# Four cross-attention layers under a planned order: rank tables of their own for the first and last batch, and two weight slabs transferred earlier

## The chip, the cores and the metric

The kernel runs on one core of a Trainium2 chip. The metric is the device time of one execution in microseconds (us). The engines are TensorE (PE, with its weight loads listed apart as PEld), VectorE (DVE), ScalarE (ACT), GpSimd (POOL) and SyncE (SP, whose queue issues the transfers).

## The reference

Four cross-attention layers in a row are applied to `x` (16 batches of 100 rows, 256 wide), each with the same context `ctx_1024` (16 batches of 361 rows, 256 wide) and 16 heads. All numbers are float32. Cut to what matters:

```python
# L0: heads of 16, layer norm on both sides, then a feed-forward
qn, kn = layer_norm(x, ln1), layer_norm(ctx, ln1)
x = x + softmax((qn @ wq + bq) (kn @ wk + bk)^T / 4) (kn @ wv + bv) @ wo + bo
x = x + gelu(layer_norm(x, ln2) @ w1 + b1) @ w2 + b2
# L1: heads of 64, rms norm on the query alone, no scale, raw context
x = x + softmax((rms(x) @ wq) (ctx @ wk)^T) (ctx @ wv) @ wo
# L2: heads of 64, rotary embedding of q and k, a mask on the keys, layer norm after the sum
x = layer_norm(x + softmax(mask(rope(x @ Wq) rope(ctx @ Wk)^T / 8)) (ctx @ Wv) @ Wo)
# L3: heads of 16, layer norm on both sides
x = x + softmax((ln(x) @ Wq + bq) (ln(ctx) @ Wk + bk)^T / 4) (ln(ctx) @ Wv + bv) @ Wo + bo
```

## The kernel before

The kernel is a list of works that is ordered on the host and then written out. For each of the 16 batches the function `batch(b)` adds some 561 works to a `Plan`: the context transposed (`keys_T`: `cT` raw, `zT` normalised), layer L0 (`small_heads_layer`), `feed_forward`, L1 and L2 (`large_heads_layer`), L3 (`small_heads_layer` again), and the store. Each work is one or several instructions of one engine, or of either ACT or DVE where an estimate may choose (`copied`). An attention layer goes in four units of four heads: `scores` on PE (L839), the row maximum on DVE (L894, or L888 and L891 with a mask), the exponential on ACT (L900), the reciprocal on DVE (L864), the division on POOL (L871), the transposes of the probabilities on PE (L935), their copy from PSUM on ACT or DVE (L614, L616), and the weighted sum on PE (L733).

PE works have a tile shape, called mode in the code: `col32` (four strips of 32 columns abreast: nearly all products, L733), `row64` (transposes by halves of 64 rows, and the scores of L1 and L2), `row32` (the scores of L0 and L3), and None (whole array: the folding of norm weights into projection weights at the start, L519 and L568, and one transpose at L487).

`Plan.order` walks through time by its own estimates. Of all works whose inputs are ready it picks the one that starts earliest; equal starts go by rank. A PE work of another mode than PE's present one counts `keep[mode]` ns later while the present run of that mode is shorter than `run[mode]` ns, and earlier by `pull` times the PE work at hand in its mode:

```python
w.rank = w.batch * ORDER["lag"] - w.tail
if w.batch >= 0:
    w.rank = w.rank + ORDER["batch"][w.batch] + ORDER["place"][w.place]
...
if engine == "PE" and start < free_at["PE"] + ORDER["window"]:
    m = mode if set_now else w.modes[0]
    at_hand[m] = at_hand.get(m, 0.0) + busy
```

Here `start` is never before `free_at["PE"]`, `place` is the number of the work within its batch, and `tail` the longest chain of estimates behind it. What comes out is a fixed order of instructions for each engine, buffers and PSUM banks included. Each engine then runs its own list strictly in that order and waits wherever an input is late.

The transfers at the start are a chain (`load`, `load_const`, `load_slab`, `load_inputs`): SP issues them in the order in which they are written. The weights come as 12 slabs of 1 MB: 0 is L0's four projections, 1 and 2 are `w1` and `w2`, 3 to 6 are L1's wq, wk, wv and wo, 7 to 10 L2's, 11 L3's four. `rows` are five bias and norm rows, `cst` the rotary tables, `crow` the column vectors. Each slab is issued at L426; the context at L398 and L402, into one buffer `ctxr` that all batches share; `x` at L403; the mask at L416. Two works wait for `rows` early: the addition at L574 on DVE, and through it the first residual row of L0 on POOL (L1000).

Of the kernel before, what the change touches and what calls it, by code (L numbers as in the profile page):

```python
# [18 lines left out]
B, S, E = 16, 100, 256  # L19
# [12 lines left out]
for _name, _w in (  # L32
# [11 lines left out]
SLABS = (  # L44
    ("L0_xattn_wk", "L0_xattn_wv", "L0_xattn_wq", "L0_xattn_wo"),
    ("L0_xattn_w1",), ("L0_xattn_w2",),
    ("L1_xattn_wq",), ("L1_xattn_wk",), ("L1_xattn_wv",), ("L1_xattn_wo",),
    ("L2_xattn_Wq",), ("L2_xattn_Wk",), ("L2_xattn_Wv",), ("L2_xattn_Wo",),
    ("L3_xattn_Wq", "L3_xattn_Wk", "L3_xattn_Wv", "L3_xattn_Wo"),
)  # L50

ORDER = {
    "lag": 329100, "pull": 7.0, "window": 0,
    "keep": {None: 5720, "row64": 350, "row32": 60, "col64": 4920, "col32": 4770},
    "run": {None: 0, "row64": 22810, "row32": 33110, "col64": 63830, "col32": 0},
    "batch": (-388000, 3000, 0, 0, 0, 0, 0, 0, 0, 0, 0, 0, 0, 0, 75500, -1018000),
    "place": [  # L60
        100 * k for k in (
        1788, 2147, 158, -655, -3660, -3678, -2864, -2202, 107, -3757, -3737, -2474, -6828,
        -7159, -6429, -769, -7090, -5897, -2734, -7751, -4511, -3850, -6654, -4642, -4482,
        -5346, -1898, 2595, -228, -444, -1077, -3621, -2420, -4476, -6306, -9158, -8069, -6006,
        -6446, -5152, -5925, -9187, -6281, -10716, -8043, -8908, -6734, -8414, -9577, -12471,
        -5956, -6155, -10918, -12687, -6524, -7417, -6968, -2206, -1022, -442, -455, -1136,
        -2296, -853, -1376, -601, -1207, -1840, 1341, -965, -1984, -3436, -983, -70, -1962,
        -308, -474, -1148, -2199, -415, 539, -44, -2289, -1348, -2217, -2483, 1649, -1589, -48,
        696, 1885, -105, 1108, -3136, 2296, 2261, -5257, -5446, -5535, -7310, -2216, -2756,
        -1279, -3966, 91, 72, -2289, -1637, -3654, -1230, -2781, -1130, 3999, 260, -460, -3123,  # L70
        -3075, -3185, 46, 1463, -4241, -4207, -2879, 377, -1894, -1072, -1487, -4901, -3613,
        -5484, -4750, -2583, -4378, -3249, -684, 1881, -2295, 6, -4275, -2714, -1398, -1067,
        104, 878, -633, -877, -70, 4307, -129, -1409, -7268, -876, -534, 37, 274, 2712, 2005,
        667, -383, 2192, 1954, -1158, -2545, -4879, -1718, 1071, 6135, 6999, 3972, 2354, 3233,
        1740, 23, 3538, 2458, 5060, -3364, -1285, -1996, -3442, -1454, -1733, 3264, -2782,
        -8386, 850, -638, -3875, -3486, -3922, -4750, -4633, -2049, -6108, -1229, -2781, -3686,
        -1451, -1172, -737, 2568, 1316, 5887, 2353, 432, 1063, 3355, 1611, 6911, 3359, -1272,
        471, 758, -3387, -4259, -244, -1565, -733, -1162, -665, 1469, -5644, -2369, -2467,
        -1133, -3934, -4444, -2937, -6670, -5590, -8380, -10655, -6731, -4637, -5076, -4059,
        -3451, -4805, -5454, -3113, -4724, 2806, -3339, 2422, 3428, 807, 2546, -23, -641, 1012,  # L80
        1005, 534, 5580, 2620, 1990, 1001, -1243, 1291, 4604, 5568, 3408, 842, -954, -3671,
        -2620, 85, -856, -4166, -9442, -5661, -1103, -588, -3921, -3608, -3730, 492, 1219, -144,
        392, 2013, 4590, 7120, 8002, 4805, 4640, -42, 3885, 3005, 5141, 3205, 3474, 4285, 5881,
        6503, 4010, 5003, 4359, 6006, 5431, 5577, 3067, 4246, 8605, 3685, 7642, 6505, 1444,
        2688, 1704, 373, 3065, -2188, 66, -2348, -3742, -576, 1795, -1133, -123, 353, 1264,
        -186, -3119, -6662, 3188, -2888, -2292, 639, -2200, -544, 3192, -2158, 268, 3976, 6005,
        2305, 2809, 1883, -2100, 3932, 3267, 4051, 4427, 5327, 5654, 6007, 7398, 1836, 4762,
        1273, 3327, 1747, 1882, 5151, 1055, 1284, -952, -703, -2974, -2900, 925, -4076, -1021,
        3029, -3569, 89, -700, -1127, 2089, -1480, 2484, 2990, 2248, -1452, 494, 2456, 841,
        -1167, -472, -998, -1941, -4850, -2206, -2817, -3790, -5666, -3510, -1965, -2311, -5292,  # L90
        -5354, -4528, -6920, -7546, -6247, -4195, -347, -1590, -2503, -5174, -5611, -2342, -254,
        -6432, -5406, -3715, -714, -1257, 679, 1808, 3757, -507, 2782, 93, 1915, 1124, -2501,
        -1632, 2528, -5366, -1885, -3098, -7585, -9522, -10769, -8421, -11233, -6607, -8773,
        -9422, -2724, -3769, -4192, -4443, -4468, -5791, -4103, -3810, -781, -5155, -2771, 414,
        -1459, -2334, -1027, -2813, -5985, -3939, -7212, -3270, -4409, -2012, -4946, -5630, 827,
        -6312, -1161, -2028, -1786, 1600, -917, -2390, 1068, 1539, 3314, -634, 3761, 2764, 6969,
        3668, -5275, -1551, -1593, -5718, -3450, 3167, 4367, 4831, 5443, 6356, 3460, 376, -1230,
        -2843, -2595, -4621, -6268, -4694, -2912, -1704, -2369, -634, -4432, -993, -2880, -899,
        -428, -4599, -6793, -2902, -6740, -6610, -2330, -263, 2256, 1828, 1882, 1805, 1066,
        4514, 1473, 739, -2476, -1257, -3998, 2747, 713, 4018, 3384, 4954, 2476, 1679, -3033,  # L100
        -682, -1921, -1131, 4768, 1129, 1216, -1441, 3923, 4051, 1136, 3547, 1612, 1261, -4001,
        -3191, -1679, 691, -338, 6706, 4913, 3905, 4065, -504, 145, -2018, -654, -6952, -1397,
        -1334, -2478, -1894, -1645, -2680, 241, 934, 1107, 1565, -3853,
        )
    ],
}


# [43 lines left out]
class Plan:  # L152
# [62 lines left out]
    def order(self):  # L215
# [6 lines left out]
        for w in self.work:  # L222
            w.rank = w.batch * ORDER["lag"] - w.tail
            if w.batch >= 0:
                w.rank = w.rank + ORDER["batch"][w.batch] + ORDER["place"][w.place]
        free_at = {e: 0.0 for e in ("PE", "ACT", "DVE", "POOL", "SP")}
        mode, run, table = None, 0.0, None
        ready = sorted((w.rank, w.index) for w in self.work if not w.n_after)
# [4 lines left out]
        while len(done) < len(self.work):  # L233
            held, able, at_hand = set(), [], {}
            for _, i in ready:
                w = self.work[i]
# [22 lines left out]
                for e, occ, lat in w.engines:  # L259
# [5 lines left out]
                    if cost is None or s + lat < cost - 1:  # L265
                        engine, cost, start, busy = e, s + lat, s, occ
                if engine == "PE" and start < free_at["PE"] + ORDER["window"]:
                    m = mode if set_now else w.modes[0]
# [12 lines left out]
            _, start, end, w, e, occ, set_now = best  # L281
            if e == "PE":
                run = run + occ if set_now else occ
# [34 lines left out]
def tile_xattn_layers(  # L318
# [65 lines left out]
    plan = Plan(slots)  # L384
# [27 lines left out]
    def load_mask(b):  # L412
        mu = plan.buf("mask", f"mask_{b}")

        def issue(_):
            nc.sync.dma_start(out=mu.ap, in_=mask[b : b + 1, :].to_broadcast([P, SK]))  # L416

        if b < 1:
            load([("SP", 200.0, 4000.0)], issue, [mu])
        else:  # L420
            plan.add([("SP", 100.0, 4000.0)], issue, writes=[mu])
        return mu

    def load_const(dst, src, us, name):
        b = plan.buf(None, name)
        load([("SP", us * 1e3, us * 1e3 + 3000.0)], lambda _: nc.sync.dma_start(out=dst, in_=src), [b])  # L426
        return b

    w, slab_of = {}, {}

    def load_slab(i, pieces=1):
        t = const.tile([P, 2048], F32, name=f"slab{i}")
        names = SLABS[i]
        n, wide = len(names), 2048 // pieces
        for k in range(pieces):
            cols = slice(k * wide, (k + 1) * wide)
            part = load_const(t[:, cols], slabs[i, :, cols], 2.5 / pieces, f"slab{i}_{k}")
            for name in names[k * n // pieces : (k + 1) * n // pieces]:
                slab_of[name] = part
        for k, name in enumerate(names):  # L440
            part = t[:, k * (2048 // n) : (k + 1) * (2048 // n)]
            kc = 8 if n == 1 and name[-2:].lower() in ("wo", "w2") else 2
            w[name] = part.rearrange("p (c n) -> p c n", c=kc)
# [5 lines left out]
    loads, masks = {}, {}  # L449
# [4 lines left out]
    crow_b = load_const(crow, colvecs, 0.1, "crow")  # L454
    load_slab(0, 2)
    cst_b = load_const(cst, consts, 1.0, "cst")
    rows_b = load_const(rows, rowvecs.partition_broadcast(P), 1.7, "rows")
    plan.batch = 0
    masks[0] = load_mask(0)
    plan.batch = -1  # L460
    load_slab(1)
    plan.batch = 1
    loads[1] = load_inputs(1, 1000.0, 5000.0)
    plan.batch = -1
    for i in range(2, len(SLABS)):
        load_slab(i)
    row = {name: rows[:, i, :] for i, name in enumerate(ROWS)}
    parity = cst[:, 0:2]
# [932 lines left out]
```

## Time and profile before

| what | value |
|---|---|
| median of 3 runs | 1950.47 us (1947.33 to 1952.12) |
| the profiled execution | 1949.26 us, span 1947.5 us |
| instructions | 99714 |
| PE busy | 1920.4 us (99%) in 43881 matmuls |
| DVE, ACT, POOL busy | 1294.9, 1179.8, 1048.2 us |
| mean granted clock of PE | 0.994 |
| read from memory | 21.92 MB |

The span is the time from the first to the last instruction; some 1.8 us lie around it. "Idle before" is the time in which an engine stood still before an instruction, with what ended it. The granted clock is PE's share of its full clock in a stretch. A busy PE in this page is one with a matmul anywhere in flight, so a change of tile shape, in which the array empties, counts as busy.

### The profile page before, as it was taken

What the parts mean: (1) busy time and instruction counts of PE and PEld (TensorE: products, weight loads), DVE (VectorE), ACT (ScalarE), POOL (GpSimd) and SP (SyncE); (2) the same over time, 40 slices, a digit from 0 to 9 for tenths busy, and PEclk for the clock granted to TensorE, in tenths of its full rate; (3) what the DMA queues carried; (4) which work ended last, traced back from release to release, by engine and by line L of the source; (5) the groups of instructions that cost most, each with busy time, mean ns of one, the idle gap of its engine ahead of it and who ended that gap; (6) DMA issues with size and microseconds to landing.
All of it is one profiled execution on the core that took longest, in us unless ns stands there. A gap on an engine that the chain in (4) does not pass through costs nothing.

```text
span 1947.5 us, 99714 instructions
## 1 busy us (share of the span) xinstructions
PE 1920.4 (99%) x43881; PEld 1272.2 (65%) x43881; DVE 1294.9 (66%) x4497; ACT 1179.8 (61%) x3425; POOL 1048.2 (54%) x1680
## 2 busy tenths in 40 slices
PE   8999999999999999999999999999999999999997
PEld 4666666575766757667575675767667576675756
DVE  5556666666676666667666676666676666775766
ACT  4646656675665756656566566655666466565636
POOL 5354455555556555455645555455555555555564
PEclk9999999999999999999999999999999999999997
DMA  7000000000000000000000000000000000000000
GB/s 303 3 3 14 5 12 8 3 14 5 12 8 3 14 5 14 5 3 15 5 14 5 12 8 3 15 5 12 8 3 15 5 12 7 3 15 4 4 3 7
DMA packets 14730, 29.94 MB, mean 15 GB/s; under 512 B 3362, under 2 KB 12376, under 8 KB 12888
## 3 DMA queue, kind: packets, MB, share of 16 engines
q1 hardware_dynamic: 14296, 23.56, 3.7%
q8 instruction: 344, 5.64, 1.2%
q14 instruction: 90, 0.74, 0.1%
HBM read 21.92 MB, written 1.64 MB: 12 GB/s over the span
## 4 chain that ended last, share of the span: by engine, by line
PE 94%; DVE 3%; POOL 2%; DMA 1%; issue 0%; ACT 0%; SPq 0%; POOLq 0%; DVEq 0%; ACTq 0%
PE ps L733 68%; PE ps L839 13%; PE ps L935 10%; DVE prob L894 2%; POOL prob L871 1%; PE ps L674 1%; PE ps L761 1%; DMA slab<-slabs_dram 1%; DMA mask<-mask_dram 0%; ACT prob L900 0%; PE ps L716 0%; SPq L426 0%; DVE prob L888 0%; DVE pT L616 0%; DVE two L891 0%
## 5 line engine op out<-in xcount | busy, mean ns | idle before, releaser
L871 POOL TENSOR_SCALAR prob<-prob,two 100x361 f32<-100x361 f32 x1024 | 568.6, 573 | 607.9 <-DVE two L864 384.8
L900 ACT ACTIVATE prob<-prob,two 100x361 f32<-100x361 f32 x1024 | 603.0, 593 | 124.3 <-DVE prob L894 73.8
L894 DVE TENSOR_SCALAR_CACHE_REDUCE prob<-ps 100x361 f32<-100x361 f32 x768 | 374.7, 531 | 171.9 <-PE ps L839 112.5
L733 PE MATMUL ps<-slab,cT 128*32 128x512 f32 (+1 forms) x3072 | 366.6, 595 | 0.0
L733 PE MATMUL ps<-cT,slab 128*32 128x361 f32 x4096 | 344.6, 468 | 0.7 <-DMA slab<-slabs_dram 0.7
L839 PE MATMUL ps<-kT,qT 32*100 32x181 f32 (+3 forms) x4096 | 303.7, 329 | 1.4 <-ACT pT L614 0.9
L935 PEld LDWEIGHTS ps<-ident,prob 36*128 36x128 f32 (+1 forms) x6144 | 216.0, 139 | 95.7 <-POOL prob L871 43.5
L614 ACT COPY pT<-ps 128x384 f32<-128x384 f32 (+1 forms) x508 | 223.6, 493 | 88.5 <-PE ps L935 69.5
L839 PEld LDWEIGHTS ps<-kT,qT 32*100 32x100 f32 (+1 forms) x4096 | 228.7, 164 | 72.6 <-issue 42.1
L935 PE MATMUL ps<-ident,prob 36*128 36x36 f32 (+1 forms) x6144 | 243.0, 227 | 7.7 <-POOL prob L871 7.2
L614 ACT COPY v<-ps 128x512 f32<-128x512 f32 (+1 forms) x131 | 76.6, 585 | 268.1 <-PE ps L733 163.5
L616 DVE COPY pT<-ps 128x384 f32<-128x384 f32 (+1 forms) x260 | 146.4, 575 | 134.3 <-PE ps L935 131.2
L733 PEld LDWEIGHTS ps<-cT,slab 128*32 128x32 f32 x4096 | 122.9, 109 | 148.5 <-issue 132.9
L900 ACT ACTIVATION_READ_ACCUMULATOR prob<-prob,two 100x1 f32 x1024 | 194.6, 190 | 0.0
L733 PEld LDWEIGHTS ps<-slab,cT 128*32 128x32 f32 (+1 forms) x3072 | 86.0, 107 | 140.0 <-issue 127.9
L888 DVE TENSOR_TENSOR prob<-ps,cap 100x361 f32<-100x361 f32 x256 | 125.7, 527 | 65.2 <-PE ps L839 41.0
L792 POOL TENSOR_TENSOR sw<-sw,rot 128x361 f32<-128x361 f32 x128 | 105.5, 825 | 105.3 <-DVE sw L788 102.3
L733 PE MATMUL ps<-pT,v 128*32 128x100 f32 (+1 forms) x6144 | 155.5, 250 | 2.7 <-DVE pT L616 2.3
L733 PEld LDWEIGHTS ps<-pT,v 128*32 128x32 f32 (+1 forms) x6144 | 136.3, 110 | 25.1 <-issue 12.3
L800 POOL TENSOR_TENSOR kT<-kT,sw 128x361 f32<-128x361 f32 x128 | 122.9, 961 | 6.0
L733 PE MATMUL ps<-xT,slab 128*32 128x100 f32 x5120 | 124.4, 250 | 1.5 <-DVE xT L696 1.0
L891 DVE TENSOR_REDUCE two<-prob 100x1 f32<-100x361 f32 x256 | 124.7, 518 | 0.0
(105 smaller groups left out, 2325.6 us busy)
## 6 DMA issues: line engine op xcount, KB each, us to landing
slab<-slabs_dram SPq DMA_DIRECT2D x11, 1024.0 KB
ctxr<-ctx_dram SPq DMA_DIRECT2D x16, 256.0 KB
ctxr<-ctx_dram SPq DMA_DIRECT2D x16, 105.0 KB
x<-x_dram SPq DMA_DIRECT2D x16, 100.0 KB
out_dram<-x SPq DMA_DIRECT2D x16, 100.0 KB
slab<-slabs_dram SPq DMA_DIRECT2D x2, 512.0 KB
mask<-mask_dram SPq DMA_DIRECT2D x16, 45.1 KB
rows<-rowvecs_dram SPq DMA_DIRECT2D x1, 640.0 KB
```

The lines of the kernel that those rows point to most:

```text
L614: nc.scalar.copy(dst(), src())
L616: nc.vector.tensor_copy(dst(), src())
L733: nc.tensor.matmul(out_f(at + t, at + t1), lhsT=lhsT[:, t:t1], rhs=rhs, start=start, stop=stop, tile_position=(0, at + t),)
L792: nc.gpsimd.tensor_tensor(a, a, wide(sin()), ALU.mult)
L800: nc.gpsimd.tensor_tensor(dst_f(dst.ap), dst_f(dst.ap), sw.ap[:, :n], ALU.add)
L839: nc.tensor.matmul(banks[h].ap[:S, k0:k1], lhsT=self.q_of(h), rhs=self.k_of(h)[:, k0:k1], start=(k0 == 0), stop=(k1 == SK), skip_group_che ...
L871: nc.gpsimd.tensor_scalar(p.ap[:S, :SK], p.ap[:S, :SK], rsum.ap[:S, j : j + 1], 1.0, ALU.mult, ALU.mult,)
L888: nc.vector.tensor_tensor(p(), bank.ap[:S, :SK], self.cap.ap[:S, :], ALU.min)
L891: nc.vector.tensor_reduce(neg_max.ap[:S, 0:1], p(), AX.X, ALU.max, negate=True)
L894: nc.vector.tensor_scalar(p(), bank.ap[:S, :SK], -1.0, None, ALU.mult, ALU.min, accum_out=neg_max.ap[:S, 0:1],)
L900: nc.scalar.activation(p(), p(), AF.Exp, bias=neg_max.ap[:S, 0:1], scale=1.0 if masked else -1.0, accum_out=sums.ap[:S, j : j + 1],)
L935: nc.tensor.transpose(out[:, c, :], probs[h].ap[q0:q1, c * KP : (c + 1) * KP], ident[q0:q1, q0:q1],)
```

## The change

It changes host-side tables and the order of the first transfers; no instruction's work is changed.

- All scalars of `ORDER` but `window` are new, and the 561 values of `place`, which are common to all batches.
- A new entry `ends` holds 561 values for batch 0 and 561 for batch 15, and `order` adds them, times 100, to the rank of the works of these two batches.
- Slabs 4 and 5, L1's key and value weights, are transferred right after `cst`, ahead of `rows`, slab 1 and the second batch's context. The first batch's mask moves from behind `rows` to behind slab 6. The rest go in the order 2, 3, 6, mask, 8, 9, 7, 10, 11.

```diff
 ORDER = {
-    "lag": 329100, "pull": 7.0, "window": 0,
-    "keep": {None: 5720, "row64": 350, "row32": 60, "col64": 4920, "col32": 4770},
-    "run": {None: 0, "row64": 22810, "row32": 33110, "col64": 63830, "col32": 0},
-    "batch": (-388000, 3000, 0, 0, 0, 0, 0, 0, 0, 0, 0, 0, 0, 0, 75500, -1018000),
+    "lag": 281400, "pull": 6.35, "window": 0,
+    "keep": {None: 4180, "row64": 280, "row32": 710, "col64": 3610, "col32": 5250},
+    "run": {None: 3260, "row64": 33260, "row32": 18740, "col64": 46890, "col32": 300},
+    "batch": (-614500, -19500, 0, 0, 0, 0, 0, 0, 0, 0, 0, 0, 0, 0, 6000, -863500),
     "place": [
         100 * k for k in (
-        1788, 2147, 158, -655, -3660, -3678, -2864, -2202, 107, -3757, -3737, -2474, -6828,
...
+        1530, 2179, 1302, -155, -3146, -3119, -1447, -50, 2198, -4316, -4647, -2582, -7311,
...
         )
     ],
+    "ends": {
+        0: (
+            -360, -553, -1511, 2397, 964, 789, -725, 912, 2373, -371, 41, 464, 1613, 1142, 2683,
...
+        ),
+        B - 1: (
+            -371, -1335, -481, -1165, -930, -1671, -1347, -2091, -2430, -759, -268, -240, -1197,
...
+        ),
+    },
 }
...
                 w.rank = w.rank + ORDER["batch"][w.batch] + ORDER["place"][w.place]
+                if w.batch in ORDER["ends"]:
+                    w.rank += 100 * ORDER["ends"][w.batch][w.place]
...
     cst_b = load_const(cst, consts, 1.0, "cst")
+    for i in (4, 5):
+        load_slab(i)
     rows_b = load_const(rows, rowvecs.partition_broadcast(P), 1.7, "rows")
-    plan.batch = 0
-    masks[0] = load_mask(0)
-    plan.batch = -1
     load_slab(1)
     plan.batch = 1
     loads[1] = load_inputs(1, 1000.0, 5000.0)
     plan.batch = -1
-    for i in range(2, len(SLABS)):
+    for i in (2, 3, 6):
+        load_slab(i)
+    plan.batch = 0
+    masks[0] = load_mask(0)
+    plan.batch = -1
+    for i in (8, 9, 7, 10, 11):
         load_slab(i)
```

## The prediction

> **What bounds the kernel now.** I read the page first, then TensorE's (PE's) timeline of the first 60 us and of the last, the queue of SP, and last the table by stretches for the end. The page gives PE's total and the chain of waits by engine.
>
> ```profile
> PE 1920.4 (99%) x43881; PEld 1272.2 (65%) x43881; DVE 1294.9 (66%) x4497; ACT 1179.8 (61%) x3425; POOL 1048.2 (54%) x1680
> ...
> PE 94%; DVE 3%; POOL 2%; DMA 1%; issue 0%; ACT 0%; SPq 0%; POOLq 0%; DVEq 0%; ACTq 0%
> ```
>
> PE is idle for 1947.5 - 1920.4 = 27.1 us and no other engine is busy for over two thirds. So a new order can only close PE's gaps, shorten the stretches of slow clock, or change how often PE's tile shape changes. The timeline of PE (start, length, line, form, count, and in brackets the idle time before) prices all three:
>
> ```profile
> 8.29 3.54 PE L519 MATMUL ps<-colt,slab 128*128 128x1 f32 x16 [1.67 <-DMA slab<-slabs_dram]
> ...
> 17.48 4.35 PE L733 MATMUL ps<-zT,slab 128*32 128x361 f32 x32 [0.73 <-DVE zT L616]
> ...
> 30.30 1.42 PE L733 MATMUL ps<-cT,slab 128*32 128x361 f32 x16 [0.66 <-DMA slab<-slabs_dram]
> ...
> 32.81 5.36 PE L733 MATMUL ps<-slab,cT 128*32 128x512 f32 x48
> ...
> 39.36 1.92 PE L733 MATMUL ps<-slab,cT 128*32 128x512 f32 x16
> 41.10 1.22 PE L733 MATMUL ps<-pT,vs 128*32 128x100 f32 x48
> 42.25 0.87 PE L839 MATMUL ps<-kT,qT 32*100 32x181 f32 x16
> 43.05 1.92 PE L733 MATMUL ps<-slab,cT 128*32 128x512 f32 x16
> ...
> 50.95 1.95 PE L519 MATMUL ps<-colt,slab 128*128 128x1 f32 x16
> ```
>
> Four column strips run abreast, so x16 is four passes. A pass of 512 columns costs (5.36 - 1.92) / 8 = 0.43 us, which is 0.84 ns a column; by that 361 columns cost 0.30, 256 cost 0.21, 181 cost 0.15 and 100 cost 0.085. The block at 41.10 (12 passes of 100, 1.02 us) is followed after 1.15 us, so the change from columns to 32-row tiles costs 0.12; the scores at 42.25 (four steps of 181, 0.61) are followed after 0.80, so the change back costs 0.19.
>
> The whole span then adds up. Column passes are 768 of 512, 1280 of 361, 512 of 256 and 5632 of 100: 330 + 384 + 108 + 482 = 1304 us. Transposes are 3488 pairs at 0.062 (a block of 36 lasts 1.33 and one of 24 lasts 0.96 in the same timeline, so 0.37 for six pairs): 216. Scores are 128 units of 0.61 and 128 of 1.22: 234. With the folds this is some 1760 us at full clock. Idle time takes 27. Slow clock takes about 16: the same 16 fold matmuls last 3.54 at 8.29 and 1.95 at 50.95, so up to 21 us, where the records of a full clock begin, PE's 12.8 busy us hold some 6 of loss; the end holds 10 (below). What is left, 1947.5 - 1760 - 27 - 16 = 144 us, falls on the changes of tile shape, of which I count 822 in the trace: 0.175 us each, inside the 0.12 to 0.19 read above.
>
> The queue of SP shows why the key weights of the second layer land at 30.3 us, ending an idle 0.66:
>
> ```profile
> 16.60 0.38 SPq L398 DMA_DIRECT2D ctxr<-ctx_dram  x1
> ...
> 17.93 10.11 SPq L426 DMA_DIRECT2D slab<-slabs_dram  x10
> ```
>
> SP issues in order, and ten slabs stand behind the second context, whose buffer comes free at 16.6. In the table by stretches the DMA share is 0.99 from 9 to 12 us, 0.55 from 12 to 15 and 0.10 from 15 to 17.5: a hole of about 3.5 us.
>
> The table of the end (columns: stretch, length, busy us of PE, PEld, DVE, ACT, POOL with counts, granted clock, DMA share, GB/s):
>
> ```profile
> 1891.50:1894.90 3.40, 3.40 (x49) 3.02 (x39) 2.25 (x8) 1.27 (x4) 1.74 (x4) 0.50 0.02 5
> 1894.90:1918.80 23.90, 18.82 (x560) 14.95 (x556) 19.91 (x78) 17.10 (x55) 10.66 (x20) 1.00 0.01 3
> 1918.80:1929.00 10.20, 9.15 (x144) 7.49 (x147) 6.44 (x27) 7.06 (x23) 6.31 (x12) 0.50 0.01 2
> 1929.00:1935.90 6.90, 5.38 (x126) 3.92 (x128) 6.23 (x27) 5.74 (x19) 4.79 (x9) 0.99 0.06 17
> 1935.90:1947.50 11.60, 7.67 (x124) 4.94 (x120) 2.69 (x7) 2.46 (x8) 1.91 (x4) 0.50 0.04 11
> ```
>
> PE is busy 3.40 + 9.15 + 7.67 = 20.2 us at half clock, a loss of 10.1. Its idle time from 1888 us on is 13.8. So the end wastes about 24 us, the head 9.1 idle + 6 slow, and the 1790 us between hold 4.2 us of idle, 3.6 of it transposes waiting for POOL's division.
>
> **The change part by part.** The scalars first. With window 0 the sum `at_hand` is always empty, because no start lies before the time PE is free; `pull` multiplies nothing, so 7.0 to 6.35 costs 0. No work has mode col64: 0. Every column work lasts over 0.3 us, so a run of 300 ns holds nothing that 0 did not: 0. The longest stretches of row64 and row32 in the trace are 3.7 and 2.2 us, far under 18.7, so both `keep` always act: row64 goes from 350 to 280 ns, and row32 from 60 to 710. The first lets PE leave transposes a little sooner; the second can hold PE for 0.7 us only where more scores are about to start, and in the trace no two of the 128 small-head score blocks stand together. Bounds: one change of shape more or fewer per batch, 16 x 0.175 = 2.8 us either way; taken at 0.
>
> Mode None: PE begins in it, and until 3.26 us of such work are done any other work counts 4.18 us later. The planner can now put the first fold before the transposes of the first context (0.97 us at 5.64 in the trace, inside the wait for the first slab). Then they come after 8.29 + 3.54 and their time is uncovered: 0 to +1.0 us, taken at +0.7.
>
> Transfers: slabs 4 and 5 (2.1 MB) are issued at about 4.5 us, ahead of `rows`, which with the first slab still goes by the 303 to 378 GB/s of the first slices: 5.5 to 7 us. They land by some 18 us instead of 30, in part through the hole. So the keys and values of the second layer, 32 passes of 0.30 and 24 of 0.43 us or 20 us of work, can fill PE from then on: the 0.66 idle goes, likely also the 0.73 at 16.75. If the stretch from 14 to 18 us is then whole, the clock rises about 3.4 us (the length of the short slow stretch at 1891.5) earlier: 1.7. Against this `rows`, landed by 13.35 in the trace, comes 5.5 to 7 us later. The addition at L574, at 14.69 on DVE, waits for it, and behind it stand L1107 and the copies of zT, which feed the first scores at 21.76: 0 to +4, taken at +0.6 since PE has the keys meanwhile. The same cover carries the second context, some 3 us later; slab 3 (to be scaled at 28.24) lands 5 us later, but its queries come after the first feed-forward; slab 1, too. The mask goes behind slab 6, and only the third layer reads it: 0, and POOL's three steps for `rot` (2.2 us) leave the head. Head in sum: -0.66 - 0.73 - 1.7 + 0.7 + 0.6 = about -2 us, bounds -5 to +4.
>
> Tables: the common table moves each of the 561 ranks by 148 us about a mean of -42 (worked out from the diff), and lag drops from 329.1 to 281.4 us, so that two neighbouring batches are mixed more closely. The trace shows no such order. The number of changes per sixteenth of the span is 49 to 55; it is 54 in the first and 55 in the last, 51 or so between. Two fewer everywhere is 16 x 2 x 0.175 = -5.6, three more is +8.4; I take -2, close to the rows there are.
>
> The own table of the last batch can move its third and fourth layers against those of batch 14. Now both finish together: from 1918.8 on PE has only the last scores. ACT needs 16 x 0.78 = 12.5 us for the last layer of one batch and POOL 16 x 0.573 = 9.2, while the stretch from the last queries (1919) to the end lasts 28.5. Bounds: all of the shortfall of ACT's 12.5 plus some 8 of latency against 28.5 gives -8 with another 6 of slow clock, -14; nothing gained is 0, and a table that puts them further apart from their cover adds as much as one stretch, +5. I take a quarter of the 24, -6.
>
> How the clock follows gaps decides half of this term. In the trace half clock begins at 1891.5 after one gap of 2.26 us (1888.69 to 1890.95), and at 1918.8 after gaps of 0.98, 1.01 and 0.49 us. So each gap closed also buys clock: of the -6, some -3.5 is idle and -2.5 clock. The Trainium skill (TensorE: Matmul & The Clock Gate, section "Why this matters for your kernels") says that only gaps above about 3 us bring the slow clock back; by that these short gaps would not matter, and the clock part would be nothing.
>
> Sum: -2 - 2 - 6 = -10 us on the profiled execution's 1949.3 (span 1947.5 + 1.8 around it), 1939.3; that execution lies 1.2 below the median of the runs, so 1940.
>
> **The rivals.** First, slower: more changes of shape. A closer mix of batches and a row64 hold of 280 ns make PE leave transposes sooner. Each change costs 0.175 us in the middle, where nothing is idle to hide it. Against a gain of 3 at the ends, 50 more changes (three per batch, +8.8) give +5.8, the bound of slower; five per batch give 1950.5 + 14 - 3 = 1961. For it: the middle has no slack, and PE follows the order strictly. Against it: the count hardly varies from batch to batch. It decides from three per batch.
>
> Second, no change: the early transfers do not do what they are for, and the end stays. PE is idle only 1.4 us between 8.3 and 60, so early weights give it nothing but another order, and the last batch is bound by its chain of softmax steps, not by rank. Then -2 at the head and -1 at the end: 1947.5. For it speaks that the gap at 30.30 is but 0.66; against it, 13.8 idle us at the end.
>
> Third, a large gain: two changes fewer per batch and the end cut by 14: -2 - 6 - 14, 1928.
>
> **How the numbers follow.** A measurement of this kernel tells about 0.3% (5.9 us) from no change. Forecast (1933 to 1944): 0.45, and the large gain 0.12, make faster 0.57. The second rival, 1944.6 to 1956.3: 0.18. The first, above: 0.25. The range from 1926 (large gain with one us of head more) to 1959 (four changes more per batch, 11.2, less 3) leaves a tenth at each end; the forecast's own range is 1933 to 1944.
>
> **What would show it.** Right: the slabs of the second layer issued before 6 us and matmuls on them before 20; idle PE below 22 us in all, below 10 after 1885; less time at half clock in the last 60 us; 790 to 822 changes of shape. Wrong: over 860 changes; DVE at L574 held past 20 us with PE idle behind it; idle PE in the middle above 8 us; or an end with the same three slow stretches.

## The result and the profile after

The changed kernel takes 1937.09 us (median of 4 runs, 1936.76 to 1940.13) against 1949.03 for the kernel before on the same chip: a ratio of 0.9936, 95% interval 0.9921 to 0.9951, so 12 us less where 10 were forecast. Its profiled execution lasts 1937.01 us with a span of 1935.2, 12.3 below the span before. The page, in the lines that answer to those of before:

```profile
PE 1914.6 (99%) x43881; PEld 1268.0 (66%) x43881; DVE 1294.5 (67%) x4502; ACT 1170.2 (60%) x3418; POOL 1045.9 (54%) x1682
...
PE 97%; DVE 1%; POOL 1%; ACT 0%; issue 0%; DMA 0%; SPq 0%; POOLq 0%; DVEq 0%; ACTq 0%
```

PE's idle time fell from 27.1 to 20.6 us and its busy time by 5.8, with the same 43881 matmuls. The timeline of PE at the head (start, length, line, form, count, idle before):

```profile
8.46 3.55 PE L616 MATMUL ps<-colt,slab 128*128 128x1 f32 x16 [2.82 <-DMA slab<-slabs_dram]
...
12.18 0.88 PE L858 MATMUL ps<-ident,ctxr 64*128 64x64 f32 x12
...
16.61 1.92 PE L830 MATMUL ps<-slab,cT 128*32 128x512 f32 x16
18.36 1.40 PE L830 MATMUL ps<-zT,slab 128*32 128x361 f32 x16
...
52.18 1.95 PE L616 MATMUL ps<-colt,slab 128*128 128x1 f32 x16
...
56.67 1.52 PE L936 MATMUL ps<-kT,qT 32*100 32x181 f32 x10 [0.58 <-ACT rT L711]
```

The first fold stands ahead of the transposes of the first context (L858), so the gap in front of it has grown from 1.67 to 2.82 us. From 8.46 to 56 us PE stands still for 0.03 us in all. The first product with slab 5 starts at 16.61, and the records of a full clock begin at 15.67 instead of 21.0 us (ahead of its first record the table by stretches reads 1.00 as well, though the fold at 8.46 takes 3.55 us and the one at 52.18 takes 1.95); a slow stretch of 3.4 us begins at 56.6. SP's queue shows the two slabs, and `rows` behind them:

```profile
4.52 2.14 SPq L517 DMA_DIRECT2D slab<-slabs_dram  x2
6.70 0.69 SPq L517 DMA_DIRECT2D rows<-rowvecs_dram  x1
```

The end by stretches (columns as before: length, busy us of PE, PEld, DVE, ACT, POOL, granted clock, DMA share, GB/s):

```profile
1885.00:1903.20 18.20, 15.99 (x469) 13.04 (x466) 15.06 (x60) 13.33 (x43) 9.16 (x17) 1.00 0.02 5
1903.20:1916.90 13.70, 11.22 (x188) 9.29 (x184) 9.20 (x39) 8.10 (x27) 7.20 (x14) 0.50 0.01 1
1916.90:1923.70 6.80, 5.48 (x123) 4.03 (x120) 5.68 (x23) 5.42 (x18) 3.84 (x7) 1.00 0.07 19
1923.70:1935.20 11.50, 6.99 (x117) 4.71 (x112) 3.40 (x10) 2.91 (x9) 2.20 (x4) 0.50 0.04 10
```

One of the three slow stretches is gone, and the other two hold 18.2 busy us instead of 20.2. They are as long as the three were, 13.70 + 11.50 = 25.2 us.

To see where the 12 us come from, I add up the work of PE's matmuls in their order, each at its price at full clock, and read at what time the same amount of work is done. That splits each span into a head (the first 50 us of work), a middle (the next 1650) and an end, all in us of the profiled executions, the planned-order runs below included:

| kernel | head | middle | end | span |
|---|---|---|---|---|
| before | 69.3 | 1777.6 | 100.6 | 1947.5 |
| after | 67.0 | 1771.5 | 96.8 | 1935.2 |
| old_order_early_slabs | 73.6 | 1776.3 | 99.9 | 1949.8 |
| new_order_later_slabs | 75.0 | 1771.1 | 95.6 | 1941.8 |
| new_tables_old_transfers | 73.5 | 1784.9 | 96.2 | 1954.6 |
| common_tables_alone | 72.8 | 1781.0 | 120.6 | 1974.4 |
| no_table_last_batch | 68.0 | 1772.6 | 120.4 | 1961.0 |

So the head gave 2.4, the middle 6.1 and the end 3.8 us. Each row is one execution. Between executions of one order the same split moves by 1.4 us in the head (after, clock_filled_end and clock_filled_end_more, which start alike) and by up to 2.8 us in the middle, so the 6.1 stands clear of that and the 2.4 less so. The experiments ask what each of these hangs on.

### The profile page after: what moved, and what is told of

Same layout as the page of the kernel before. It is cut to its first block, busy times and chain, and to the rows that moved or that the text cites. A ratio compares the mean times of both kernels' runs of the same rounds, so it can differ in the third digit from the quotient of the medians.

```text
span 1935.2 us, 99776 instructions
## 1 busy us (share of the span) xinstructions
PE 1914.6 (99%) x43881; PEld 1268.0 (66%) x43881; DVE 1294.5 (67%) x4502; ACT 1170.2 (60%) x3418; POOL 1045.9 (54%) x1682
## 4 chain that ended last, share of the span: by engine, by line
PE 97%; DVE 1%; POOL 1%; ACT 0%; issue 0%; DMA 0%; SPq 0%; POOLq 0%; DVEq 0%; ACTq 0%
PE ps L830 70%; PE ps L936 14%; PE ps L1032 11%; PE ps L771 1%; PE ps L858 1%; PE ps L813 0%; ACT prob L997 0%; DMA slab<-slabs_dram 0%; DVE prob L991 0%; PE ps L616 0%; PE ps L665 0%; POOL prob L968 0%; DVE pT L713 0%; DVE prob L985 0%; POOL kT L897 0%
## 5 line engine op out<-in xcount | busy, mean ns | idle before, releaser
L711 ACT COPY pT<-ps 128x384 f32<-128x384 f32 (+1 forms) x521 | 231.1, 492 | 93.4 <-PE ps L1032 77.4
L1032 PE MATMUL ps<-ident,prob 64*128 64x64 f32 (+1 forms) x6144 | 240.8, 227 | 1.5 <-ACT pT L711 0.8
L713 DVE COPY pT<-ps 128x384 f32<-128x384 f32 (+1 forms) x247 | 137.4, 573 | 130.9 <-PE ps L1032 128.7
L711 ACT COPY v<-ps 128x512 f32<-128x512 f32 (+1 forms) x119 | 69.7, 586 | 245.6 <-PE ps L830 161.8
```

The lines of the kernel that those rows point to most:

```text
L711: nc.scalar.copy(dst(), src())
L713: nc.vector.tensor_copy(dst(), src())
L1032: nc.tensor.transpose(out[:, c, :], probs[h].ap[q0:q1, c * KP : (c + 1) * KP], ident[q0:q1, q0:q1],)
```

## The experiments

**The transfers, with every engine's order kept.** Two kernels keep a planned order as it is and only issue slabs 4 and 5 (`tagged`) elsewhere. In old_order_early_slabs the order is that of before:

```diff
+        early = [tagged[4], tagged[5]]
+        done = [x for x in done if x not in early]
+        at = done.index(tagged["cst"]) + 1
+        done[at:at] = early
```

> The order of before is kept for every engine; only the two transfers of L1's key and value weights are issued right after cst, ahead of rows. Theory (early weights alone give a fixed order next to nothing): the 0.66 us wait at 30.3 us goes, DVE at L574 waits for rows until about 17.5 us instead of running at 14.7, and qT behind it comes later: -0.7 and 0 to +2, so 1948 to 1951 us, and middle and end agree with before to 1 us. Rival (the transfers themselves are the gain at the head): 2.4 us less after 50 us of PE work, 1946.5.

Measured: 1950.58 us, ratio to before 1.0012 (1.0003 to 1.0021). The early transfers alone make the old order slower, as the first theory had it but by more: 4.3 us in the head. PE's timeline and DVE's waits (us in total, times, longest):

```profile
16.10 0.59 PE L763 MATMUL ps<-ident,ctxr 64*128 64x64 f32 x12
21.58 4.79 PE L735 MATMUL ps<-zT,slab 128*32 128x361 f32 x32 [4.89 <-DVE zT L618]
```

```profile
DVE cap L1312 <- DMA mask<-mask_dram: 5.4, 1, 5.4
```

DVE stands for 5.4 us, at the step that reads the mask, which in that order comes ahead of the addition of `rows`; the copy of zT stands behind it, and PE waits 4.89 us for that. The mask is the smaller part of this: by the records of their landing `rows` came at 17.8 us and the mask at 18.9, so DVE would have stood for some 4.2 us for `rows` alone. The changed kernel moves the mask behind slab 6, and its planned order reads it later; there DVE waits for `rows` (3.3 us), while PE has the products of slab 5.

In new_order_later_slabs the order is that of after, and the two slabs go behind `rows` and slab 1:

```diff
+        late = [tagged[4], tagged[5]]
+        done = [x for x in done if x not in late]
+        at = done.index(tagged[1]) + 1
+        done[at:at] = late
```

> The order of after is kept for every engine; only the two slabs 4 and 5 are issued behind rows and slab 1 instead of ahead of them, 1.7 MB later. Theory (the new order leans on them, since its first product of raw context and value weights is at 16.6 us): PE waits there for the 1.7 MB at 300 to 430 GB/s, 4 to 5.6 us, and the clock rises one step later; +4 to +7 us, 1941 to 1944. Rival (other work hides it): within 1 us of after.

Measured: 1943.56 us, ratio 0.9975 (0.9965 to 0.9984), some 7 us above after, with all of it in the head (75.0 against 67.0).

```profile
21.02 3.64 PE L832 MATMUL ps<-slab,cT 128*32 128x512 f32 x16 [3.63 <-DMA slab<-slabs_dram]
```

PE waits 3.63 us for slab 5, its first product runs at half clock (3.64 us for what takes 1.92), and the full clock comes at 25.3 us. The new order needs the early slabs, and the early slabs cost the old order time: in the head neither is worth anything without the other. Over the whole span the new order with late slabs still keeps a part of the gain (0.9975 against 0.9936).

**The tables by parts, planned anew.** In common_tables_alone the kernel before gets the new scalars, `lag` and offsets included, and the common table; in new_tables_old_transfers the kernel after gets the old order of transfers; in no_table_last_batch it loses the table of batch 15:

```diff
-        B - 1: (
-            -371, -1335, -481, -1165, -930, -1671, -1347, -2091, -2430, -759, -268, -240, -1197,
...
```

> Before with the new scalars, lag, batch offsets and common table, but the old order of transfers and no tables of their own for the first and last batch. Theory (the 6 us that the middle loses come from the common table, head and end from the other two parts): middle as in after, head and end as in before or a few us worse; 1943 to 1950. Rival (the tables work only together): the middle too is as long as before or longer, 1950 or more.

Measured: 1975.56 us, ratio 1.0140 (1.0126 to 1.0154).

> After with all its tables, planned anew with the old order of transfers. Theory (only the head changes): the 2.4 us of the head are lost, and 1 to 3 more, because the batch 0 table expects the early weights; middle and end as in after; 1939 to 1943. Rival (any other start makes another plan all the way): the middle changes by several us as well.

Measured: 1955.04 us, ratio 1.0035 (1.0023 to 1.0048).

> After without the table of its own for the last batch, planned anew; all else as in after. Theory (that table moves only the end): head and middle as in after to 1 us up to where the last batch begins, the end 4 us longer or more; 1941 to 1950. Rival (the end is bound by the last softmax chain whatever the ranks): within 1 us of after.

Measured: 1962.80 us, ratio 1.0062 (1.0049 to 1.0075).

In the first two the rival holds. The middle of common_tables_alone is 3.4 us longer than before, that of new_tables_old_transfers 7.3 us, though both have the table that the gain of the middle would have come from. Another start gives another plan all the way: the second of them differs from after only in which transfers come first, and has 754 changes of tile shape from 100 to 1700 us of work instead of 736. In the third the theory holds for the place and not for the size: the middle stays to 1.1 us, and the end is 23.6 us longer, 1962.8 us in all where 1941 to 1950 were expected. Its waits of PE from 1850 us on say at what:

```profile
PE ps L989 <- POOL prob L925: 9.1, 6, 3.4
PE ps L728 <- POOL z L704: 7.8, 2, 4.3
```

The last batch's third layer then ends alone, and PE waits for POOL's divisions and for its normalised rows with nothing left to do. So the table of the last batch repairs an end that the common table spoils, and goes a little beyond; it is not an end of before with 4 us taken off. The table of the first batch was not taken out by itself.

Of the scalars, `pull`, `keep` and `run` of the column modes, and `run` of the row modes changed by themselves in the old kernel give the same instruction lists on all five engines, and so does `keep` of row32 by itself: worth exactly 0, as argued from the code. The `run` of mode None is not among them: by itself it changes the lists of all engines but SP. The `keep` of row64 by itself could not be tried: with 280 in the old tables the walk comes to a state in which no work finds its buffers.

**What shortened the middle.** Between two blocks of different shape, the time from the first matmul of the one to the first of the other, less the block's own work, is the price of the change plus any wait. The median price by kind is the same in both kernels to 5 ns or less: columns to row32 or transposes 0.141 to 0.143 us, transposes back to columns 0.143 to 0.145, row32 to anything 0.193, scores of 64 rows to transposes 0.070. What lies above these medians I take as waiting, even where an earlier matmul still in flight hides it from the idle column. From 100 to 1700 us of work:

| | before | after |
|---|---|---|
| changes of shape | 723 | 736 |
| their price, by medians | 112.5 us | 114.3 us |
| waits above the medians | 11.8 us | 4.0 us |

In the whole trace the count is 822 in both; the first 50 us of work have 34 before and 26 after.

The visible part of the waits is in PE's waits from 60 to 1850 us, first before:

```profile
PE ps L935 <- POOL prob L871: 3.6, 13, 0.3
```

and after, where the transposes no longer wait for POOL's division:

```profile
PE ps L830 <- issue: 0.3, 1, 0.3
```

The old order with half of the division takes those waits away in another manner:

```diff
-                        p.ap[:S, :SK], p.ap[:S, :SK], rsum.ap[:S, j : j + 1], 1.0,
+                        p.ap[:S, :SK // 2], p.ap[:S, :SK // 2], rsum.ap[:S, j : j + 1], 1.0,
```

> Before with POOL dividing only the first 180 of 361 columns of each probability tile, so that the output is not the reference's; the order is kept. Theory (the middle of before is lengthened by transposes that wait for POOL, visibly 3.6 us, and some 2.4 us more that hide behind matmuls in flight): the middle gets 3.6 to 6 us shorter, as much as the new order gained. Rival (the other inputs are late by as much): the visible waits move to DVE and ACT, less than 2 us.

Measured: 1942.39 us, ratio 0.9959 (0.9946 to 0.9972). The part from 100 to 1700 us of work is 3.4 us shorter (1724.3 to 1720.9), and the waits above the medians fall from 11.8 to 9.1. No wait for POOL, DVE or ACT is left among PE's waits from 60 to 1850 us, so the visible 3.6 us were the division's and have not moved to another input. The 3.4 us are a little under the lower bound of the theory, and not much more than the 2.8 us between executions of one order; the run as a whole gains more, because its end is some 3 us shorter too. The other waits that the new order removed, 4 to 5 us, I have not told apart: what they waited for stays open.

**The clock at the end.** These are PE's gaps in after around the start of its slow stretch at 1903.2:

```profile
1900.51 0.85 PE L936 MATMUL ps<-kT,qT 32*100 32x181 f32 x10 [0.70 <-ACT pT L711]
...
1902.99 0.33 PE L771 MATMUL ps<-ident,z 64*128 64x64 f32 x4 [0.97 <-POOL z L747]
1904.43 1.56 PE L830 MATMUL ps<-xT,slab 128*32 128x100 f32 x32 [1.11 <-ACT xT L791]
1907.37 1.54 PE L936 MATMUL ps<-kT,qT 32*100 32x181 f32 x16 [1.37 <-DVE qT L1204]
```

In clock_filled_end PE multiplies the identity by itself in four gaps of after, into a bank that the next work overwrites; three of them are the 0.97, 1.11 and 1.37 us above, and the 0.70 stays:

```diff
+            for _ in range(fill.get((work.batch, work.place), 0)):
+                bank = slots["ps"][1] if work.batch < 0 else next(x.ap for x in work.bufs if x.cls == "ps")
+                nc.tensor.matmul(bank[:, :P], lhsT=ident, rhs=ident, start=True, stop=True)
```

> After with 16 products of the identity with itself added on PE in four gaps of the end (ahead of the last batch's query transposes, query projection, first scores and last weighted sum). Theory (gaps of about 1 us bring the half clock from 1903 to 1917, which costs 5.6 us): that stretch gets shorter or goes; -2 to -5 us at the end. Rival (the rule that only gaps over 3 us matter, or that transposes do not hold the clock up): the slow stretch stays, and the added work costs 0 to +1.5 us.

Measured: 1934.43 us, ratio 0.9923 (0.9909 to 0.9938). The stretches of the end, to be held against the second one of after:

```profile
1903.20:1916.90 13.70, 12.72 (x262) 10.17 (x266) 11.74 (x50) 10.05 (x32) 8.47 (x16) 1.00 0.01 2
1916.90:1923.70 6.80, 4.31 (x108) 3.13 (x96) 5.61 (x23) 5.97 (x19) 4.22 (x8) 0.95 0.07 19
```

The whole slow stretch from 1903 is gone. In after only the gaps of 0.70 and 0.97 us lie ahead of it; those of 1.11 and 1.37 come when the clock is already at half. That filling is the cause rests on more than one pair: in all five profiled executions of this order with nothing added at the end (after, new_order_later_slabs, transposes_before_fold, clock_filled_head, clock_wide_head) a slow stretch of 10 to 14 us begins 29 to 33 us before the end, and in none of the three with the end filled. Which gap starts it is not shown: in transposes_before_fold it begins at 1902.7, when only the gap of 0.70 has passed, and in clock_filled_end the clock stays full after the same gap. By the end the time gained is 3.2 us, not the 5.6 of the lost clock: PE now waits 0.71 and 0.42 us for POOL, where after has 0 and 0.21, and 0.82 for ACT as there. By the run times alone clock_filled_end can't be told from after. A fuller filling, 23 products ahead of eight works:

> clock_filled_end with eight more... in all 23 products of the identity ahead of eight works of the end, so that the gaps of 0.3 to 0.8 us between 1910 and 1925 are filled too. Theory (each short gap in a window lowers the clock): the remaining stretch of half clock from 1923 to 1930 goes as well, 3 us of loss, of which 1 to 2 reach the end; 1932.5 to 1933.5. Rival (the end is now bound by POOL, ACT and DVE): no faster than clock_filled_end, 1934 to 1936.

Measured: 1932.15 us (1930.20 to 1937.09), ratio 0.9911 (0.9896 to 0.9927), the fastest here, though its interval still meets that of after. In its profiled execution the end is at full clock as long as PE works:

```profile
1901.00:1915.00 14.00, 13.66 (x278) 10.90 (x274) 12.05 (x52) 10.06 (x32) 8.56 (x16) 1.00 0.01 2
1915.00:1929.00 14.00, 9.85 (x200) 7.32 (x192) 7.15 (x28) 7.14 (x22) 5.53 (x10) 0.97 0.06 18
```

**The head.** In transposes_before_fold the first context's transposes go back into the gap ahead of the fold:

```diff
+        first, shift = at[0, 2], at[-1, 19]
+        done.remove(first)
+        done.insert(done.index(shift), first)
```

> After with one work moved: the transposes of the first context stand ahead of the first fold again, all else in the order of after. Theory (mode None cost 0.7 to 1.0 us there): 0.9 us of transposes at half clock go into the 2.8 us gap, all that follows comes 0.9 earlier, 1936.2. Rival (slab 5, which feeds the product at 16.6, lands only just then): PE waits for it instead, 0.

Measured: 1936.83 us, ratio 0.9933 (0.9917 to 0.9950): no difference. In its profile the fold itself starts later, at 9.10 us, PE waits another 0.40 before L665, and the full clock comes at 18.5; so one execution with a later start can't tell whether the order of these two costs anything, and 0.9 us is too little for the run times. Two kernels then keep PE busy while it waits for the first transfers: clock_filled_head with 13 products of 128 moving columns, clock_wide_head with four of 512 (the identity read four times over):

> After with 13 products of the identity with itself added on PE, into a bank that is overwritten afterwards: 7 ahead of the first transpose and 6 ahead of the first fold, where PE waits for transfers. Theory (the clock follows how busy PE has been in the last 3.4 us): full clock from about 9 us instead of 15.7, the 3.75 us of clock loss there fall under 1; -1 to -3 us. Rival (slab 5 binds at 16.6): the clock rises early, but PE waits for the slab; within 0.5 us of after.

Measured: 1934.79 us (1932.66 to 1937.98), ratio 0.9926 (0.9911 to 0.9942). It can't be told from after, and the mechanism that I had expected isn't there:

```profile
1.63 3.36 PE L1451 MATMUL ps<-ident 128*128 128x128 f32 x14 [1.63 <-POOL ident masks.py:199]
...
8.25 3.41 PE L616 MATMUL ps<-colt,slab 128*128 128x1 f32 x16
```

PE is busy from 1.63 us but for 0.3, yet the fold still takes 3.41 us, and the full clock comes at 16.8.

> After with four products of 512 moving columns (the identity read four times) added on PE where it waits for transfers at the start: two ahead of the first transpose, two ahead of the first fold. In clock_filled_head products of 128 moving columns kept PE busy from 1.6 us and the full clock still came at 16.8 us. Theory (what counts is the share of time in which columns stream, and a weight load per 128 columns leaves too little of it): full clock before 10 us, -1.5 to -3 us. Rival (the identity's zeros do not count, or something else holds the clock): full clock at 14 to 17 us as before, within 1 us of after, or 0.6 later by the last added product.

Measured: 1936.99 us, ratio 0.9930 (0.9917 to 0.9943).

```profile
7.88 1.92 PE L616 MATMUL ps<-colt,slab 128*128 128x1 f32 x16 [0.23 <-DVE mv L726]
...
16.40 3.19 PE L830 MATMUL ps<-slab,cT 128*32 128x512 f32 x16 [0.51 <-DMA slab<-slabs_dram]
```

With 512 columns the clock is full from 5.3 us and the fold takes 1.92. Nothing of it reaches the end of the head: PE now stands 1.98 us for POOL's normalised context, 0.51 for slab 5, and the half clock is back from 15.6 to 19.0. So a fuller clock alone wins nothing in the head: PE then waits for POOL and for the landing of slab 5.

The forecast of an early clock came true, but the reason given for it does not follow. At half clock the added products start every 0.214 us with 128 columns and every 0.855 us with 512, which is 1.67 ns a column in both, so the weight load per 128 columns takes no streaming time away. What also differs is where the clock's steps fall. In every trace here its switches lie whole multiples of 3.41 us apart (in after 15.67, 56.63, 60.05 and 1903.24 us). Counted back from its switch, clock_wide_head has a step from 1.92 to 5.34 that is all products; clock_filled_head has none, since its step from 3.15 to 6.56 holds the gap of 0.3 us and the next ends in the fold. Against the place speaks head_and_end_together below, where wide products bring the full clock after a step (2.50 to 5.91) with a gap of 0.2 us in it. With one execution of the narrow products the runs don't decide between the two.

The last kernel put all this together, slab 5 ahead of slab 4, its first product ahead of the second transposes, and both fillings:

```diff
+        i, j = done.index(at[-1, 4]), done.index(at[-1, 5])
+        done[i], done[j] = done[j], done[i]
+        product, turn = at[0, 158], at[0, 10]
+        done.remove(product)
+        done.insert(done.index(turn), product)
```

> The edits that the runs point to, together: the 23 products at the end as in clock_filled_end_more, the four wide products at the head as in clock_wide_head, and in the head slab 5 (values) issued ahead of slab 4 (keys), with the first product of slab 5 moved ahead of the transposes of the normalised context. Theory (the head was held by the landing of slab 5 at 16.4 us, and the clock alone could not help): slab 5 lands some 3 us earlier, its first product starts at 13 to 14 us under a full clock, and 1 to 3 us are won beyond clock_filled_end_more: 1929 to 1931. Rival (rows, which the first scores need by way of DVE, hold the head at 17.5 us whatever comes before): nothing beyond clock_filled_end_more, 1932.

Measured: 1933.73 us (1933.07 to 1934.76), ratio 0.9924 (0.9911 to 0.9938).

```profile
14.05 1.92 PE L830 MATMUL ps<-slab,cT 128*32 128x512 f32 x16 [1.83 <-DMA slab<-slabs_dram]
15.90 0.59 PE L858 MATMUL ps<-ident,ctxr 64*128 64x64 f32 x12
17.45 1.42 PE L830 MATMUL ps<-zT,slab 128*32 128x361 f32 x16 [0.95 <-ACT zT L711]
```

The product starts 2.6 us earlier and the scores at 20.5 instead of 21.4. DVE waits 6.2 us for `rows`, until 18.0, so in the head the rival is nearer to what happened than the theory. The end is slow again, with PE busy:

```profile
1917.40:1927.60 10.20, 10.11 (x132) 7.85 (x132) 3.67 (x11) 3.49 (x12) 2.46 (x5) 0.50 0.01 3
```

So the fillings don't guarantee the clock: with the same 23 products one profiled execution has no slow stretch while PE works at the end and the other has one of 10 us. Its median lies below that of after, with intervals that overlap, and not below that of clock_filled_end_more.

## Why the prediction was right, and where it was not

The total was right, 1937.1 against 1940 in a range of 1926 to 1959, and the bound was read rightly: PE remains the busy engine, with the same matmuls. That the total came so close is in part luck: the middle gave 4 us more than forecast, by another mechanism, and the end 2 us less. By its own terms:

- **Head**, predicted -2, measured -2.4. The two gaps of 0.66 and 0.73 us went, and the clock rose 5.3 us earlier instead of 3.4, worth 2.7. How much of that is the new order is open: in clock_filled_end and clock_filled_end_more, which start with the same instructions, the full clock comes at 18.3 and 16.8 us and not at 15.7. The fold did go ahead of the transposes and the gap grew by 1.15 (0.7 was taken); undoing it won nothing that could be measured. The two slabs landed at 13.5 and 16.0 us, not at 18, and `rows` at 17.5 instead of 13.3, so 4.2 us later and not 5.5 to 7. Not foreseen were the slow stretch at 56.6 us, which costs 1.7, and 8 changes of shape fewer in the first 50 us of work. DVE's wait for `rows` came (3.3 us, until 17.5), and PE was covered, as assumed. That the mask stood ahead of `rows` on DVE was missed; in the old order with early slabs it adds 1.1 us to the wait for `rows`.
- **Scalars**, predicted 0: right for all that could be tried.
- **Middle**, predicted -2 from fewer changes of shape, measured -6.1. This step had the wrong mechanism. Changes rose by 13 from 100 to 1700 us of work, which costs 1.8 us, and are 822 in the whole trace as before; waits fell by 7.8. I had read 4.2 us of idle time in the middle as all the waiting there was; another 7.6 were inside the 0.175 us that I took for the price of a change. The medians by kind would have shown them as waits.
- **End**, predicted -6, measured -3.8: the term was mis-sized. Idle time fell by 2.6 (13.8 to 11.2) as against 3.5, and the clock part was 1.0 (20.2 to 18.2 busy us at half clock) as against 2.5. Two slow stretches stayed, together as long as the three before.
- **The clock rule.** The end's clock part rested on short gaps bringing the half clock, and they can: it begins at 1903.2 us in after when gaps of 0.70 and 0.97 us have passed in the 3.4 us before, and at 1902.7 in transposes_before_fold with one of 0.70. Gaps are not all of it. In head_and_end_together it begins at 53.7 us after 3.4 us in which PE stood still for 0.02, and which hold the second fold, 16 matmuls of one column in 1.95 us. In before a gap of 1.40 us (1896.7 to 1898.1) left the clock full. The prediction's own case at 1918.8 counts a gap of 0.49 us of which only 0.2 lay ahead of the switch. The Trainium skill (TensorE: Matmul & The Clock Gate, section "Why this matters for your kernels") advises against idle gaps of PE above about 3 us between bursts of matmuls, since one window of idle brings the slow clock back. The measurement decides against reading it as the prediction did, that shorter gaps would not matter.
- **The rivals.** More changes of shape is what the parts show when they are planned alone (754 and 758 in the middle, 1955 and 1976 us); the tables together kept to 736. The early transfers by themselves were not merely worth nothing, as the second rival had it, but cost time.
- **The signs.** Those for being right came in part: slabs issued before 5 us with matmuls on them at 16.6, 20.6 us idle in all, 822 changes. Idle PE after 1885 is 10.5 us where under 10 was named, and the time at half clock in the last 60 us has not become less. None of the signs for being wrong came. Two slips of arithmetic decide nothing: PE is idle 1.8 us between 8.3 and 60, not 1.4, and the large gain with one more us of head gives 1927.5, not 1926.

## What to carry to other kernels

When a planner's tables are searched for one plan, the parts of such a change cannot be priced one by one: here each part that was tried alone, or the whole without one of its parts, was slower than the kernel before or lost most of the gain. A share of 99% busy says little about waits: compare the step between blocks with its own median by kind; what lies above it is most likely waiting, which the idle column need not show. Where a bound engine's clock follows its activity, a gap costs more than its length, but a fuller clock gains only up to the next late input.

## What the runs showed of the hardware

- The clock switches in steps: within each of the 14 traces all switches lie whole multiples of 3.41 us apart, and the place of the steps differs from execution to execution (full clock at 15.7, 16.8 and 18.3 us with the same start).
- The full clock did not come with 6 us of products of 128 columns on PE from 1.63 us on (16.8 us), but it came at 5.3 and 5.9 us with products of 512. Whether the width or the place in the step decides is open.
- In four traces (clock_filled_end, clock_wide_head, transposes_before_fold, head_and_end_together) the half clock begins at 53.7 to 56.5 us after 3.4 us in which PE stood still for 0.02 us; each of these stretches holds the 16 matmuls of one column.
- Changing the tile shape costs 0.14 us from columns to rows of 32 or transposes and from transposes back, 0.19 us out of 32-row tiles, and 0.07 us or less between the scores and the transposes of 64 rows, nearly the same in both kernels.
- Executions of one order differ by up to 2.8 us in the middle with the same instructions: the same 1600 us of work took 1718.3 us in after and 1716.8 in clock_wide_head, 1719.6 in clock_filled_end.
